# Output tiles in a pool of their own, the second unit's queries in the scores' banks, and a half's row products earlier

## The chip, the core and the metric

The kernel runs on one core of one Trainium2 chip. The metric is the device time of one execution in microseconds (us); lower is better. The engines are PE (TensorE), DVE (VectorE), ACT (ScalarE), POOL (GpSimd) and SP (SyncE, which here issues DMAs only). They run beside each other and wait for one another by semaphores. PSUM, into which PE writes, has eight banks.

## The reference, cut to what matters

Two layers, each an attention and a feed-forward network (FFN), each followed by a residual and a layer norm; two sequences of 1024 tokens, 256 features. The first attention is grouped-query softmax attention with rotary positions, the first FFN a gated one with int8 weights. The second attention is a gated delta rule with 16 heads of 128, and the last FFN has sign weights. The change touches the end of the first FFN, and the delta rule:

```python
q = silu(dwconv_causal(x @ Wq, ...))          # 4 taps; k and v in the same way
alpha, beta = sigmoid(x @ Wa + ba), sigmoid(x @ Wb + bb)
def step(S, inp):                              # per head, over T
    err = einsum('bhvk,bhk->bhv', S, kt) - vt
    S = at[..., None, None] * S - bt[..., None, None] * err[..., None] * kt[:, :, None, :]
    return S, einsum('bhvk,bhk->bhv', S, qt)
o = (o - mu) * rsqrt(var + 1e-05) * ln_w + ln_b      # per head
o = (o * sigmoid(x @ Wg)).reshape(B, T, H * DV)
x = layernorm(x + o @ Wo)
```

## The kernel before, in words

**Stages.** The first attention takes up to about 680 us. The second half of the first FFN (blocks n = 8 to 14, two row tiles of 128 tokens each) then runs beside the key work of the delta rule's first units. From about 820 to 2010 us the delta rule's 32 units follow, some 37 us each; the last FFN runs beside the last two and behind them.

**Units.** The tokens are cut into four halves (each 512 tokens, HC = 4 chunks of 128; the names `hi`, HT = 512), the 16 heads into NS = 8 pairs (HP = 2 heads). Unit i is pair s = i mod 8 of half hi = i // 8. For a unit, `project` makes a 512-column product (two heads, six matmuls each, float32 split into high and low parts), for v, q, k and the output gate g. `conv` reads it from PSUM: ACT writes the last tap and two DVE operations (L275) add two taps; `conv_out` lets ACT write the fourth tap (`far`, L289), POOL add it (L292) and ACT apply silu. Only when `far` has read the bank is it free. `keys` does this for k, four units ahead (AHEAD), and then the decay scans (L325), the products of keys and the triangular inverse (`blocks`, `levels`: L384 and L390 on DVE, n L423, px L431 on PE). `others` does v, q, the transposed keys, the gate and the scores of the next unit. `decayed` multiplies k and q by the decays dg (POOL, L519 and L521), which a broadcast DMA loads (L214).

**The recurrence.** `recur(i)` goes over four chunks: pr is v transposed plus k times the state M (L673, L677), ACT copies it (prs, L680), pw is the inverse times prs (L688), ACT copies it (wc, L691), pm updates the state (L700, copied by DVE at L705 or added at L707), po is the output (L715, L716), which ACT copies to o.

**Finish.** `finish(i)` runs in the unit that follows unit i's own. The moments of each head (L657, L658) and a reciprocal root (om, L931 to L943, the last twelve operations on POOL) scale o (L609, three quarters of it on POOL); PE transposes it (pt, L615), ACT and DVE apply norm and gate (y, L619), POOL splits it (yh L623, yl L917), and PE multiplies by Wo (pf, 12 matmuls for two chunks). DVE adds pf to the rows `xtok` (L636). After the last pair of a half (s = NS - 1: units 7, 15, 23 and 31, so the work falls into units 8, 16, 24) the rows are normed by `layernorm` (L948 to L952) and stored on SP.

**Order.** TensorE's order is strict from the first unit on: `te.link` puts a dependency on the matmul before. The order itself is made when the kernel is built: `Places` holds generators, each yielding the place at which it goes on (UNIT = 120 places a unit), and the one with the lowest place is run next. The four places of `finish` are those of the transposes of the two heads and of the two pf products:

```python
AT_FINISH, AT_FINISH_LAST, AT_HALF = (41, 51, 101, 111), (31, 41, 71, 76), ((22, 30, 46), (1, 6, 13))
```

The other engines' orders are made by a scheduler from the dependencies, with some operations set ahead (`tc.high_priority`) or behind others (`after`).

**Memory.** `ps_p` (two banks) takes the projections, `ps_m` (two) the scores, the key products and transposes, "c" (two), "t" (one) and "l" (one) the recurrence, finish and inverse. `open_late` opens the last three and the pools "late" and "w" when the first FFN's blocks are all issued; their SBUF lies where the first FFN's tiles, its rows x among them, lay, so a first writer waits for the last reader there, the store of x.

**The start of the first unit.** `rest_of_first` loads dg of unit 0, multiplies its k and q, then runs v and q of unit 1 and both heads of key unit 4, all in `ps_p`. The last FFN block's `layernorm` uses POOL (`eng=nc.gpsimd`), then SP stores the rows (L927), then issues dg (L214).

Of the kernel before, what the change touches and what calls it, by code (L numbers as in the profile page):

```python
# [12 lines left out]
F32R = mybir.dt.float32r  # L13
# [76 lines left out]
AT_FFN = 24  # L90
AT_FINISH, AT_FINISH_LAST, AT_HALF = (41, 51, 101, 111), (31, 41, 71, 76), ((22, 30, 46), (1, 6, 13))

FFN0, FFN1, FFN1_LAST, FFN1_TAIL = 7.6, 22.0, 27.0, 40.0
# [51 lines left out]
def delta_rule(  # L145
# [24 lines left out]

    def open_late():
        pools["late"] = open_pool(right, "dlate", "right", 2)
        pools["w"] = open_pool(outer, "dw", "right")
        for name, bufs in (("c", 2), ("t", 1), ("l", 1)):
            pools[name] = open_pool(right, "ps_" + name, "right", bufs, PSUM)
# [62 lines left out]

    def project(m, i, h):
        hi, s = place(i)  # L240
        if h == 0 and ("w" + m) not in st[i]:
            st[i]["w" + m] = weights(m, s)
        wh, wl = st[i]["w" + m]
        xh, xl = halves[hi]["xh"], halves[hi]["xl"]
        pp = bank(ps_p, "p", "pp")
        hs = slice(h * P, (h + 1) * P)
        for k in range(2):
            mm3(pp, wh[:, k, hs], wl[:, k, hs], xh[:, k, :], xl[:, k, :], k == 0, k == 1)
        return pp
# [10 lines left out]
    def conv(m, i, h, pp):  # L260

        hi, s = place(i)
        n, hd = "qkv".index(m), s * HP + h
        acc = half_tile(early if m == "k" else conv_pool, m, 10 if m == "k" else 4)
        st[i][m, h] = acc

        with tc.high_priority():
            nc.scalar.activation(  # L268
                acc, pp, AF.Identity, bias=cb[:, n, hd : hd + 1], scale=cw[:, n, hd, KS - 1 : KS]
            )  # L270
            if hi % 2 == 0:
                nc.scalar.copy(halos[:, n, hd, :], pp[:, HT - KS + 1 :])  # L272

            for d in range(1, KS - 1):
                made = nc.vector.scalar_tensor_tensor(  # L275
                    acc[:, d:], pp[:, 0 : HT - d], cw[:, n, hd, KS - 1 - d : KS - d], acc[:, d:], ALU.mult, ALU.add
                )
                if m == "k" and d == 1 and solved:
                    after(made, solved[-1])
        return made  # L280
# [18 lines left out]
    def keys(i, t0):  # L299

        hi, s = place(i)
        col = halves[hi]["col"]
        pps = [project("k", i, h) for h in range(HP)]
        if i < last:
# [175 lines left out]

    def pair(m, i):

        pps = [project(m, i, h) for h in range(HP)]
        for h in range(HP):
            conv(m, i, h, pps[h])
        if i < last:
            yield AT_OUT
        for h in range(HP):
            conv_out(m, i, h, pps[h])
# [32 lines left out]

    def gate(i):
        st[i]["pg"] = [project("g", i, h) for h in range(HP)]

    def gate_rows(i):
        for h in range(HP):
            g = half_tile(pools["late"], "gt", 5)
            made = nc.scalar.activation(g, st[i]["pg"][h], AF.Tanh, scale=0.5)
# [28 lines left out]
    def rest_of_first():  # L558
# [4 lines left out]
        te.strict, te.last = True, ended[0]  # L563
        for m in "vq":
            drain(pair(m, 1))
        ks = keys(AHEAD, AT_KEYS)
        next(ks)
        lines.add(ks, next(ks), 0)

    def gate_of_first():  # L570
        gate(0)
        yield GAP
        gate_rows(0)

    def finish(i, o, m, chunks, places):

        hi, s = place(i)
        if s == 0:
            halves[hi]["x"] = load_tokens(pools["late"], hi * HC, HC)
        x = halves[hi]["x"]  # L580
        if chunks[0] == 0:
            st[i]["wo"] = []
            for part in range(2):
                t = pools["late"].tile([P, HP, E], F32R, name=f"wo{part}", tag=f"wo{part}", bufs=1)
                nc.sync.dma_start(
# [25 lines left out]
        for h in range(HP):  # L611
            yield places[h]
            pt = bank(pools["t"], "t", "pt")[:, 0 : nc_ * P]
            for c in chunks:
                te.link(nc.tensor.transpose(pt[:, (c - c1) * P : (c - c1 + 1) * P], o[:, c, h, :], ident))  # L615
            y = half_tile(pools["late"], "y", 1)[:, 0 : nc_ * P]
            with tc.high_priority():
                nc.scalar.activation(pt, pt, AF.Identity, bias=lnb, scale=lnw)
                nc.vector.scalar_tensor_tensor(y, st[i]["gt", h][:, t1], 1.0, pt, ALU.add, ALU.mult)  # L619
            yh = pools["late"].tile([P, HT], F32R, name="yh", tag="yh", bufs=2)[:, 0 : nc_ * P]  # L620
            yl = pools["late"].tile([P, HT], F32R, name="yl", tag="yl", bufs=2)[:, 0 : nc_ * P]
            with ahead():
# [21 lines left out]
    def recur(i):  # L644
# [8 lines left out]
        def moments(c):  # L653
# [6 lines left out]
            if c % part == part - 1:  # L660
# [3 lines left out]
                    i, o, m[:, chunks[0] * HP : (c + 1) * HP, :], chunks,  # L664
                    AT_HALF[c // part] if i == last else AT_FINISH_LAST if i == last - 1 else AT_FINISH,
                ), at, at if i == last else (i + 1) * UNIT)
# [178 lines left out]
    for i in range(-AHEAD, last + 1):  # L845
# [19 lines left out]
        elif 0 <= i < last:  # L865
            lines.add(others(i + 1), t + AT_ROWS, t)
        if i == 0:
            lines.add(gate_of_first(), t + AT_QUERIES)
        if i >= 0:
# [28 lines left out]
def tile_two_layers(ctx: ExitStack, tc: tile.TileContext, a, out):  # L898
# [586 lines left out]
    def open_ffn(group):  # L1485
# [20 lines left out]
        def block(n):  # L1506
# [45 lines left out]
            with tc.high_priority() if n == NT - 2 else nullcontext():  # L1552
                for i in range(2):
                    y = new("fy", [P, E], 2)
                    nc.vector.tensor_mul(y, po[i], s_down)
                    nc.vector.tensor_add(x[:, n + i, :], y, x[:, n + i, :])
                anchor["norm"] = layernorm(pool, x, n, 2, eng=nc.gpsimd)
                store_tokens(xs, n, x[:, n : n + 2, :])
# [129 lines left out]
```

## Time and profile before

| | us |
|---|---|
| median of 3 runs | 2052.26 (2052.05 to 2056.88) |
| the profiled execution, its time | 2052.92 |
| its span, first to last instruction | 2051.2 |
| mean granted clock of TensorE | 0.977 |
| 800 to 840: PE busy of 40 us | 30.7 |
| 1110 to 1165: PE busy of 55 us | 49.30 |
| 1185 to 1240 (no half ends here) | 51.72 |
| 1405 to 1460 | 45.46 |
| 1700 to 1755 | 51.33 |

The profiled execution gives the durations; 1.7 us of its time lie outside the span. In the lines, a number behind "<-" in brackets is the idle time just before an instruction, with the instruction that ended it. The line numbers are those of the kernel before. In a window of 55 us in the middle of a half PE is busy for 51.7; the three windows in which a half ends show how much PE stands there.

### The profile page before, as it was taken

To read this page: it belongs to the slowest core of one execution; us is meant where nothing else is said; L and a number is where in the kernel's file an instruction comes from. 1 tells how busy PE (TensorE), PEld (TensorE's weight loads), DVE (VectorE), ACT (ScalarE), POOL (GpSimd) and SP (SyncE) were. 2 spreads that over 40 slices of the span, in tenths; PEclk is the share of its full clock that TensorE was granted. 3 is DMA by queue.
4 is the path that set the end of the run, shared out by engine and by line. 5 is a ranking of instruction groups with operands and counts; after the bars stand their busy time and mean duration, and the time that the engine had idled before them with its cause. 6 is when DMAs were issued, how large, how long until landed. Compare 5 with 4: busy or idle time off the path is not lost.

```text
span 2051.2 us, 49222 instructions
## 1 busy us (share of the span) xinstructions
PE 1888.1 (92%) x18657; PEld 1491.8 (73%) x18657; DVE 1475.0 (72%) x3477; ACT 1266.7 (62%) x2731; POOL 1077.4 (53%) x1739
## 2 busy tenths in 40 slices
PE   5898889999998898999999899999899999999986
PEld 3454455555556787888889789888888888888775
DVE  5756666887756995676787787678678679766566
ACT  1365556566655366567676676776676766676542
POOL 4353333331124464666776656666567676665453
PEclk8999999999999999899999999999999999999997
DMA  5564443441232431443444434345434344443010
GB/s 169 165 190 133 147 131 125 149 135 55 69 77 62 116 92 55 134 123 110 127 115 116 142 99 118 115 115 137 116 101 133 114 126 109 125 135 96 18 52 22
DMA packets 312998, 229.17 MB, mean 112 GB/s; under 512 B 139640, under 2 KB 278904, under 8 KB 312760
## 3 DMA queue, kind: packets, MB, share of 16 engines
q1 hardware_dynamic: 299640, 210.73, 35.3%
q10 hardware_dynamic: 9760, 10.83, 1.6%
q0 software_dynamic: 3360, 4.46, 0.9%
q8 instruction: 147, 2.41, 0.5%
q14 instruction: 91, 0.75, 0.1%
HBM read 171.18 MB, written 51.87 MB: 109 GB/s over the span
## 4 chain that ended last, share of the span: by engine, by line
PE 57%; DVE 11%; DMA 6%; ACT 5%; POOL 4%; issue 3%; SPq 1%; DVEq 0%; ACTq 0%; POOLq 0%
PE pp L968 5%; PE pp L969 4%; PE pp L970 4%; PE ps L1342 4%; PE av L1363 4%; PE ps L1273 3%; PE pkq L508 3%; PE pm L700 2%; PE pr L677 2%; DVE at L325 2%; PE pw L688 2%; PE po L716 2%; PE po L715 2%; PE p L478 2%; PE p L471 2%
## 5 line engine op out<-in xcount | busy, mean ns | idle before, releaser
L1282 DVE TENSOR_REDUCE mx<-ps 128x4 f32<-128x1024 f32 (+1 forms) x320 | 344.2, 1111 | 130.1 <-PE ps L1273 89.3
L1346 ACT ACTIVATE es<-ps 128x512 f32<-128x512 f32 (+1 forms) x608 | 313.9, 578 | 127.2 <-PE ps L1342 116.7
L1342 PE MATMUL ps<-qT,kT 128*128 128x512 f32 (+3 forms) x768 | 219.1, 368 | 19.2 <-ACT es L1346 18.4
L1273 PE MATMUL ps<-kT,qT 128*128 128x512 f32 x576 | 200.0, 421 | 28.1 <-DVE mx L1282 18.1
L1342 PEld LDWEIGHTS ps<-qT,kT 128*128 128x128 f32 x768 | 129.6, 188 | 105.2 <-ACT es L1346 59.6
L1273 PEld LDWEIGHTS ps<-kT,qT 128*128 128x128 f32 x576 | 101.8, 191 | 88.7 <-DVE mx L1282 48.0
L289 ACT ACTIVATE far<-pp,cw 128x509 f32<-128x509 f32 x192 | 133.2, 699 | 46.6 <-DVE k L275 18.8
L1363 PE MATMUL av<-es,vaug 128*32 128x512 f32 (+3 forms) x1536 | 156.7, 496 | 0.7 <-POOL es L1349 0.7
L917 POOL TENSOR_TENSOR wfl<-wf,wfh 128x256 fp32r<-128x256 f32 x80 | 58.4, 733 | 187.2 <-ACT wfh L1006 155.9
L1349 POOL TENSOR_SCALAR_AFFINE_SELECT es<-es 128x512 f32<-128x512 f32 x128 | 80.2, 635 | 145.3 <-ACT es L1346 141.7
L275 DVE SCALAR_TENSOR_TENSOR q<-pp,cw,q 128x511 f32<-128x511 f32 (+1 forms) x128 | 93.2, 742 | 47.6 <-ACT halos L272 24.2
L275 DVE SCALAR_TENSOR_TENSOR k<-pp,cw,k 128x511 f32<-128x511 f32 (+1 forms) x128 | 92.1, 743 | 45.5 <-ACT k L268 25.0
L292 POOL TENSOR_TENSOR q<-q,far 128x509 f32<-128x509 f32 x64 | 69.3, 1085 | 97.8 <-ACT far L289 97.7
L275 DVE SCALAR_TENSOR_TENSOR v<-pp,cw,v 128x511 f32<-128x511 f32 (+1 forms) x128 | 92.2, 739 | 33.4 <-ACT v L268 18.3
L292 POOL TENSOR_TENSOR k<-k,far 128x509 f32<-128x509 f32 x64 | 77.7, 1215 | 51.2 <-ACT far L289 50.6
L519 POOL TENSOR_TENSOR k<-k,dg 128x508 f32<-128x508 f32 x64 | 82.2, 1284 | 33.0 <-PE pkq L508 29.0
L1006 ACT CAST wfh<-wf 128x256 fp32r<-128x256 f32 x80 | 32.3, 405 | 107.4 <-DMA wf<-in_w1k 35.7
L716 PE MATMUL po<-wc,at 128*128 128x128 f32 x512 | 96.8, 276 | 0.0
L680 ACT COPY prs<-pr 128x256 f32<-128x256 f32 x128 | 48.8, 381 | 77.7 <-PE pr L677 69.5
L325 DVE TENSOR_TENSOR_SCAN at<-da,d 128x512 f32<-128x512 f32 x64 | 90.1, 1448 | 0.0
L700 PE MATMUL pm<-wc,kc 128*128 128x128 f32 x448 | 77.6, 296 | 11.4 <-ACT wc L691 11.4
L688 PEld LDWEIGHTS pw<-prs,lt 128*128 128x128 f32 x512 | 76.7, 191 | 14.9 <-ACT prs L680 3.0
(323 smaller groups left out, 5916.2 us busy)
## 6 DMA issues: line engine op xcount, KB each, us to landing
wk<-w1k SPq DMA_DIRECT2D x64, 256.0 KB
da<-dec SPq DMA_DIRECT2D x64, 256.0 KB
wv<-w1v SPq DMA_DIRECT2D x64, 256.0 KB
wq<-w1q SPq DMA_DIRECT2D x64, 256.0 KB
dg<-dec SPq DMA_DIRECT2D x64, 256.0 KB
wg<-w1g SPq DMA_DIRECT2D x64, 256.0 KB
wo<-w1o SPq DMA_DIRECT2D x64, 256.0 KB
ad<-avs ACTq DMA_DIRECT2D x32, 256.0 KB
```

Of the source, the lines that this page charges most:

```text
L275: made = nc.vector.scalar_tensor_tensor(acc[:, d:], pp[:, 0 : HT - d], cw[:, n, hd, KS - 1 - d : KS - d], acc[:, d:], ALU.mult, ALU.add)
L289: made = nc.scalar.activation(far[:, w], pp[:, w], AF.Copy, scale=cw[:, n, hd, 0:1])
L292: nc.gpsimd.tensor_add(acc[:, KS - 1 :], acc[:, KS - 1 :], far[:, w])
L325: nc.vector.tensor_tensor_scan(e, dec, d1.rearrange("p c t -> p (c t)"), 0.0, ALU.mult, ALU.add), taps
L688: te.link(nc.tensor.matmul(pw[:, r], lhsT=lt[:, h * HC + c, :], rhs=prs[:, r], start=True, stop=True))
L700: te.link(nc.tensor.matmul(pm[:, r], lhsT=st[i]["kc", h][:, c, :], rhs=wc[:, r], start=True, stop=True))
L716: te.link(nc.tensor.matmul(po[:, r], lhsT=st[i]["at", h][:, t], rhs=wc[:, r], start=(M is None), stop=True))
L1273: anchor["mm"] = te.link(nc.tensor.matmul(ps[:, j - j0, :].rearrange("p (g k) -> p g k", k=P), lhsT=q_, rhs=kT[:, :, j * P : (j + 1) * P], ...
L1282: nc.vector.tensor_reduce(mx[:, it, j0 // 2, :], ps[:, 0:n, :].rearrange("p j (g k) -> p g j k", k=P), AX.XY, ALU.max)
L1342: te.link(nc.tensor.matmul(ps[:, g - g0, :], lhsT=kT[:, g, jb * P : (jb + 1) * P], rhs=qT[:, i0 : i0 + w], start=True, stop=True,))
L1346: exps.append(nc.scalar.activation(es[:, g0 : g0 + n, 0:w], ps, AF.Exp, scale=D ** -0.5))
L1363: mm = te.link(nc.tensor.matmul(av[ROW * g : ROW * (g + 1), i0 - ih * 512 : 512], lhsT=vaugs[b][:, jb, kv, :], rhs=es[:, g, 0:w], start=(j ...
```

## The change

A pool "out" is opened before "late" and takes the output side's tiles: the gate gt, the rows xtok, wo, y, yh and yl. `project`, `pair` and `gate` take a pair of pool and tag for their banks: q of unit 1 and the gate of unit 0 go to `ps_m`. `rest_of_first` projects only the first key head of unit 4; the second comes from a new stream, `first_keys`, at a place inside unit 0. The last FFN block's norm makes its reciprocal root on DVE (nine operations, L936 to L938) instead of POOL (twelve, L940 to L943), and one tap of unit 1's q is ordered behind that norm. `finish` of the last pair of the first three halves has its two row products at places 86 and 94 instead of 101 and 111.

The number of matmuls stays. On PE the order changes at four spots: two transposes (pr of unit 0's first chunk) go ahead of the second key head, and in units 8, 16 and 24 the sequence "k head, pw, pf, po of chunk 3, pf" becomes "pf, k head, pf, pw, po". On SP one load of wk goes ahead of the store of x, and the loads of wk in those three units come behind the two DMAs of the inverse.

```diff
@@ -89,6 +89,7 @@
 AT_LEVELS = 43, 53, 73, 83, 103, 113, 132, 142
 AT_FFN = 24
 AT_FINISH, AT_FINISH_LAST, AT_HALF = (41, 51, 101, 111), (31, 41, 71, 76), ((22, 30, 46), (1, 6, 13))
+AT_FINISH_ROWS = 41, 51, 86, 94
 
 FFN0, FFN1, FFN1_LAST, FFN1_TAIL = 7.6, 22.0, 27.0, 40.0
 
@@ -169,6 +170,8 @@
     ps_m = open_pool(left, "ps_m", "left", 2, PSUM)
 
     def open_late():
+
+        pools["out"] = open_pool(right, "dout", "right", 2)
         pools["late"] = open_pool(right, "dlate", "right", 2)
         pools["w"] = open_pool(outer, "dw", "right")
         for name, bufs in (("c", 2), ("t", 1), ("l", 1)):
@@ -236,13 +239,13 @@
 
         return divmod(i, NS)
 
-    def project(m, i, h):
+    def project(m, i, h, psum=None):
         hi, s = place(i)
         if h == 0 and ("w" + m) not in st[i]:
             st[i]["w" + m] = weights(m, s)
         wh, wl = st[i]["w" + m]
         xh, xl = halves[hi]["xh"], halves[hi]["xl"]
-        pp = bank(ps_p, "p", "pp")
+        pp = bank(*(psum or (ps_p, "p")), "pp")
         hs = slice(h * P, (h + 1) * P)
         for k in range(2):
             mm3(pp, wh[:, k, hs], wl[:, k, hs], xh[:, k, :], xl[:, k, :], k == 0, k == 1)
@@ -275,6 +278,8 @@
                 made = nc.vector.scalar_tensor_tensor(
                     acc[:, d:], pp[:, 0 : HT - d], cw[:, n, hd, KS - 1 - d : KS - d], acc[:, d:], ALU.mult, ALU.add
                 )
+                if m == "q" and i == 1 and d == 1:
+                    after(made, anchor["norm"])
                 if m == "k" and d == 1 and solved:
                     after(made, solved[-1])
         return made
@@ -300,7 +305,8 @@
 
         hi, s = place(i)
         col = halves[hi]["col"]
-        pps = [project("k", i, h) for h in range(HP)]
+        pps = [st[i].pop("first")] if "first" in st[i] else [project("k", i, 0)]
+        pps.append(project("k", i, 1))
         if i < last:
             st[i + 1]["wk"] = weights("k", place(i + 1)[1])
         for h in range(HP):
@@ -478,9 +484,9 @@
                     te.link(nc.tensor.matmul(p4[A, u, :], lhsT=n3[Z, u, :], rhs=lt[Z, u, Z], start=True, stop=True))
             nc.scalar.copy(st[i + n]["lt"][A, :, Z], p4[A])
 
-    def pair(m, i):
-
-        pps = [project(m, i, h) for h in range(HP)]
+    def pair(m, i, psum=None):
+
+        pps = [project(m, i, h, psum) for h in range(HP)]
         for h in range(HP):
             conv(m, i, h, pps[h])
         if i < last:
@@ -520,12 +526,12 @@
         if "q" in which:
             nc.gpsimd.tensor_mul(q, q, gs)
 
-    def gate(i):
-        st[i]["pg"] = [project("g", i, h) for h in range(HP)]
+    def gate(i, psum=None):
+        st[i]["pg"] = [project("g", i, h, psum) for h in range(HP)]
 
     def gate_rows(i):
         for h in range(HP):
-            g = half_tile(pools["late"], "gt", 5)
+            g = half_tile(pools["out"], "gt", 5)
             made = nc.scalar.activation(g, st[i]["pg"][h], AF.Tanh, scale=0.5)
             if copied:
                 after(made, copied[-1])
@@ -561,14 +567,21 @@
             for h in range(HP):
                 decayed(0, h, which)
         te.strict, te.last = True, ended[0]
-        for m in "vq":
-            drain(pair(m, 1))
+
+        for m, psum in (("v", (ps_p, "p")), ("q", (ps_m, "m"))):
+            drain(pair(m, 1, psum))
+        st[AHEAD]["first"] = project("k", AHEAD, 0)
+
+    def first_keys():
+
         ks = keys(AHEAD, AT_KEYS)
         next(ks)
-        lines.add(ks, next(ks), 0)
+        yield AT_ROWS + AT_OUT
+        yield next(ks)
+        yield from ks
 
     def gate_of_first():
-        gate(0)
+        gate(0, (ps_m, "m"))
         yield GAP
         gate_rows(0)
 
@@ -576,12 +589,12 @@
 
         hi, s = place(i)
         if s == 0:
-            halves[hi]["x"] = load_tokens(pools["late"], hi * HC, HC)
+            halves[hi]["x"] = load_tokens(pools["out"], hi * HC, HC)
         x = halves[hi]["x"]
         if chunks[0] == 0:
             st[i]["wo"] = []
             for part in range(2):
-                t = pools["late"].tile([P, HP, E], F32R, name=f"wo{part}", tag=f"wo{part}", bufs=1)
+                t = pools["out"].tile([P, HP, E], F32R, name=f"wo{part}", tag=f"wo{part}", bufs=1)
                 nc.sync.dma_start(
                     out=t.bitcast(F32),
                     in_=w1d["o", part][s * HP * P : (s + 1) * HP * P, :].rearrange("(h p) e -> p h e", p=P),
@@ -613,12 +626,12 @@
             pt = bank(pools["t"], "t", "pt")[:, 0 : nc_ * P]
             for c in chunks:
                 te.link(nc.tensor.transpose(pt[:, (c - c1) * P : (c - c1 + 1) * P], o[:, c, h, :], ident))
-            y = half_tile(pools["late"], "y", 1)[:, 0 : nc_ * P]
+            y = half_tile(pools["out"], "y", 1)[:, 0 : nc_ * P]
             with tc.high_priority():
                 nc.scalar.activation(pt, pt, AF.Identity, bias=lnb, scale=lnw)
                 nc.vector.scalar_tensor_tensor(y, st[i]["gt", h][:, t1], 1.0, pt, ALU.add, ALU.mult)
-            yh = pools["late"].tile([P, HT], F32R, name="yh", tag="yh", bufs=2)[:, 0 : nc_ * P]
-            yl = pools["late"].tile([P, HT], F32R, name="yl", tag="yl", bufs=2)[:, 0 : nc_ * P]
+            yh = pools["out"].tile([P, HT], F32R, name="yh", tag="yh", bufs=2)[:, 0 : nc_ * P]
+            yl = pools["out"].tile([P, HT], F32R, name="yl", tag="yl", bufs=2)[:, 0 : nc_ * P]
             with ahead():
                 (nc.gpsimd.tensor_copy if i < last else nc.scalar.copy)(yh, y)
                 sub_low(nc.gpsimd if i < last else nc.vector, yl, y, yh)
@@ -662,7 +675,8 @@
                 at = i * UNIT + 3 * GAP * (c + 1) + 3
                 lines.add(finish(
                     i, o, m[:, chunks[0] * HP : (c + 1) * HP, :], chunks,
-                    AT_HALF[c // part] if i == last else AT_FINISH_LAST if i == last - 1 else AT_FINISH,
+                    AT_HALF[c // part] if i == last else AT_FINISH_LAST if i == last - 1
+                    else AT_FINISH_ROWS if s == NS - 1 else AT_FINISH,
                 ), at, at if i == last else (i + 1) * UNIT)
 
         for c in range(HC):
@@ -865,6 +879,7 @@
         elif 0 <= i < last:
             lines.add(others(i + 1), t + AT_ROWS, t)
         if i == 0:
+            lines.add(first_keys(), t + AT_ROWS, t)
             lines.add(gate_of_first(), t + AT_QUERIES)
         if i >= 0:
             lines.add(recur(i), t, chain=True)
@@ -1554,7 +1569,7 @@
                     y = new("fy", [P, E], 2)
                     nc.vector.tensor_mul(y, po[i], s_down)
                     nc.vector.tensor_add(x[:, n + i, :], y, x[:, n + i, :])
-                anchor["norm"] = layernorm(pool, x, n, 2, eng=nc.gpsimd)
+                anchor["norm"] = layernorm(pool, x, n, 2, eng=nc.gpsimd if n < NT - 2 else None)
                 store_tokens(xs, n, x[:, n : n + 2, :])
             yield 0.2
 
```

## The prediction

> **What bounds the kernel now.** I read the page first: busy shares, then the span in forty slices.
>
> ```profile
> span 2051.2 us, 49222 instructions
> PE 1888.1 (92%) x18657; PEld 1491.8 (73%) x18657; DVE 1475.0 (72%) x3477; ACT 1266.7 (62%) x2731; POOL 1077.4 (53%) x1739
> PE   5898889999998898999999899999899999999986
> PEclk8999999999999999899999999999999999999997
> ```
>
> TensorE bounds the whole, in an order written out by hand. The change leaves its number of matmuls as it is, so it can only move the time in which PE stands still or runs at a lowered clock. A slice is 51 us; two stretches that the change touches are dips: slice 16 (769 to 821 us, PEclk 8), where the delta rule's first unit begins, and the half boundaries (units 8, 16, 24). The stage table and PE's waits at the transition:
>
> ```profile
> 810.00:820.00 10.00, 5.97 (x19) 4.01 (x19) 7.55 (x20) 6.06 (x13) 5.02 (x13) 0.74 0.41 122
> 820.00:830.00 10.00, 7.34 (x26) 5.69 (x25) 9.37 (x28) 3.60 (x9) 8.95 (x8) 0.50 0.99 313
> 830.00:840.00 10.00, 9.98 (x59) 8.65 (x58) 1.66 (x8) 5.00 (x16) 1.63 (x3) 0.90 0.40 93
> ```
>
> Columns: PE, PEld, DVE, ACT, POOL busy, granted clock, DMA share, GB/s. In 820 to 830 the clock is 0.50. PE's waits of 800 to 832 (sum, times, longest):
>
> ```profile
> PE pp L968 <- ACT far L289: 5.8, 3, 2.1
> PE pr L677 <- DVE M L705: 0.9, 1, 0.9
> ```
>
> PE waits three times for a projection bank that the convolution's last tap (far) still reads. The timelines of DVE, POOL and SP there name the rest:
>
> ```profile
> 813.67 1.15 DVE L952 TENSOR_SCALAR x<-x,ln 128x256 f32<-128x256 f32 x1 [1.05 <-POOL ln L943]
> 815.40 0.40 DVE L952 TENSOR_SCALAR x<-x,ln 128x256 f32<-128x256 f32 x1
> 822.59 4.02 DVE L325 TENSOR_TENSOR_SCAN at<-da,d 128x512 f32<-128x512 f32 x2
> 820.91 1.26 POOL L519 TENSOR_TENSOR k<-k,dg 128x508 f32<-128x508 f32 x1 [2.49 <-DMA dg<-dec]
> 815.83 0.36 SPq L927 DMA_DIRECT2D xs<-x  x1
> 816.29 0.90 SPq L214 DMA_DIRECT2D dg<-dec  x2
> ```
>
> The last FFN block's norm ends late (12 POOL operations at a pitch of 0.28, 809.42 to 813.64), so its store is issued at 815.83; dg is queued behind it on SP and lands at 820.87; POOL's four dg multiplications end at 827.6; DVE meanwhile is in two scans, with the copy of M (L705) behind them. The boundaries, from PE's waits:
>
> ```profile
> PE px L431 <- DVE n L423: 2.3, 1, 2.3
> PE pt L615 <- POOL o L609: 7.7, 2, 7.1
> ```
>
> The first is of 1110 to 1165, the second of 1405 to 1460. PE is busy 49.30, 45.46 and 51.33 of 55 us at the three boundaries, against 51.72 in 1185 to 1240: room of about 2.4, 6.3 and 0.4.
>
> **The change, part by part: the transition.**
>
> Pool of their own. The first prs copy (L680) no longer inherits x's store; at 821.0 the store and pr (820.04) were both behind it. Alone about 0 to 1. The tanh's gt now waits for the store, but it stands at 833 and later: nothing.
>
> Second unit's queries in ps_m. Today v and q of unit 1 and key head 0 and 1 take the two ps_p banks in turn: waits of 1.82, 1.92 and 2.11, the 5.8 above. With q in the two ps_m banks and the first key head straight behind, I add up from v's end at 806.55: q 12 matmuls at 0.235 (2.8) to 809.35, key head 0 (6, 1.4) to 810.75. All three waits go from this place. The first pr then waits for silu and taps of v, which end on POOL at 810.97 and ACT about 812.85; key head 1, moved behind it, ends at 814.5; pw, wc and pm end by 816.3 (today 823.6). That is 7 us earlier, but what comes next is pr with M of chunk 1, and it needs k multiplied by dg.
>
> Norm on DVE. Nine operations of 0.15 to 0.17 at a pitch of about 0.1 (0.9), plus two x of 0.40, replace twelve at 0.28 (3.4) that were interleaved with two adds of 1.08. The norm ends at about 810.9 rather than 815.8, the store goes then, and dg behind it at 811.4. Issue to landing took 4.6 (816.29 to 820.87) with the channel still 41% busy, so dg lands at about 816.0 to 816.5. The ordering of q's tap behind the norm costs DVE nothing, since that tap waits for ACT anyway.
>
> The dg multiplications. On POOL two at 1.26 and the next at 1.27 to 2.17: both heads of k are done at 821.3 to 821.8 (with the q between them) against 827.63. M's copies now stand ahead of the scans on DVE (about 817.4, today 826.65). So pr with M of both heads moves from 828.48 to about 821.8: gain 6.7. Two things are late next. POOL's adds of q's far taps are queued behind the dg work, ACT's far of the keys behind them, and wc of chunk 1 behind that, at about 827; and gate of unit 0, now in ps_m, must be read by ACT before pk takes the bank. They take back about 1.1: pr of chunk 2 at 830.1 rather than 835.69. **Gain 5.6.** Bounds: 3 if dg takes 2 us longer to land (the wg and wk loads are issued closer behind it; 313 GB/s at 0.99 in 820 to 830 shows the channel full) and half a us more goes to ACT; 8 if none of the 1.1 is taken back and wg runs at full clock.
>
> On that clock: matmuls of wg took 0.43 from 828 to 832 and 0.23 after, following four waits of 0.9 to 2.1 each within 20 us. The change gathers these into one wait of 4 to 5 us for dg, so I keep the twelve wg matmuls slow before and after, a difference of 0. The Trainium skill, TensorE: Matmul & The Clock Gate, section What's actually happening, says the clock halves after one idle window of about 3.4 us. By that rule the old gaps would not have throttled, which this trace contradicts (0.50), and the new one would; the sum by the rule would be about 2.4 us less gain (12 times 0.20).
>
> SP. One wk load goes ahead of the store (0.6 of issue); ps_p and PE's queue wait for neither. Nothing.
>
> **Part by part: the half boundaries.** AT_FINISH_ROWS moves both output products (pf, 12 matmuls each) of units 7, 15, 23 ahead of the following k products and pw: about 15 places, 4 to 5 us. PE's count is the same. The first pf meets yl's second head (POOL L917 ends 1120.27; PE is there at about 1118.5): a wait of 1.1 to 1.7, paid three times, but the following pf and pr would have waited on DVE partly anyway; I carry it inside the sums below. The wk loads behind d and dt on SP come ten places later and are needed a unit on: nothing. The store of the half is earlier, good for the next gates, which are not waited for.
>
> DVE is the matter: at 1130 to 1150 it is busy 10.0 of every 10 us. The scheduled order puts the row norm of the first two chunks (add, statistics, nine short operations at 0.08 pitch, two scalings at 0.40: about 3 us) ahead of the k taps. Then the head norm (om, L931 to L933) stands behind more work than today. First boundary: three v taps (2.1), L339 (0.67), two M updates (0.59), L407 (0.70), 12 short row-norm operations (1.0), two L952 (0.80), about 5.7 us more. Third: the same with a second L339 and two statistics, 6.6. Second: three taps, two L339, L407 leave, the row norm comes, 3.1 less. Behind om stand 12 POOL operations at 0.29, o (L609), then pt (L615), and PE in strict order behind pt:
>
> ```profile
> 1133.13 0.17 DVE L933 TENSOR_SCALAR om<-om 128x8 int32<-128x8 int32 x1
> 1137.83 2.48 POOL L609 TENSOR_SCALAR o<-o,om 128x128 f32<-128x128 f32 x3
> 1147.05 1.58 PE L431 MATMUL px<-n,dt 32*32 32x32 f32 x128 [2.26 <-DVE n L423]
> 1439.25 0.26 POOL L943 TENSOR_TENSOR om<-om 128x8 f32<-128x8 f32 x1
> 1439.62 2.60 POOL L609 TENSOR_SCALAR o<-o,om 128x128 f32<-128x128 f32 x3
> ```
>
> First: o ends 6 to 6.7 later, so pt, today at 1139.98 without a wait, waits some 6; the 2.26 that px waits today is swallowed, so px is 4.5 later. Third: pt 6.5 later, px's wait 0.8, so 5.8 later. Second: the om chain on POOL is no longer split by q's two adds (1435.52, 1438.21), o ends at about 1437.0 instead of 1442.2, matmuls behind a shorter wait run faster (L420 1.93 there, 1.29 at the first): 6.9 earlier. **Sum +3.4**, slower. Bounds: -7 (first and third cost 0, second gains all), +12 (first 6.7, third 6.5, clock loss of 1 each as after the 7.1 wait, second gains 2).
>
> **Sum.** The profiled run took 2052.92 (span 2051.2 and 1.7 around it), 0.66 over the median. 2052.92 - 5.6 + 3.4 = 2050.7; less 0.66, 2050.
>
> **Rivals.**
>
> Faster, boundaries lose nothing: the row norm of some 6 us runs on DVE before the taps instead of between them and px's n, where the same 6 us delay PE today; the wait only changes place. For it: all DVE work ahead of n is the same within 2 us by count. Against: the strict order has pt between. Then -5.6 - 6.9, 2040; with half the cost left, 2045.
>
> Slower, the wait for o takes the place of px's: first +6.7, third +6.5, about 1 each for the clock that falls after such a wait, second 0 because POOL's adds of v still stand in the om chain, transition only 3 because dg lands late. +15.2 - 3 = +12.2, 2064. It decides if the boundaries cost over 12 with the full gain, or 9 with 3. For it: PE's 7.1 wait for L609 at the second boundary shows that the chain does end there. Against: work moved ahead of om is absent later.
>
> No gain at the start: the 5.8 of bank waits turns into a wait for dg or for wc, whose landing does not move. Then +3.4: 2055.7. Against: the store's place on SP is plain.
>
> **How the numbers follow.** A difference of 0.3% (6.2 us) is about what a measurement can tell: 2046 to 2058. Forecast case 0.36, its own range 2046 to 2056; no gain at the start 0.04; boundaries free 0.34, 2038 to 2046; wait for o 0.26, 2058 to 2066. The eight-in-ten range cuts the ends of the last two: 2040 to 2062. Faster 0.34, within 0.40, slower 0.26.
>
> **What would show it.** Right: no wait of pp L968 at 806 to 818; store issued near 811, dg landing near 816; pr of chunk 1 with M at 822, of chunk 2 at 830; at the first and third boundary a PE wait of 5 to 6 at pt L615 for POOL o L609, and the second's 7.1 down to 2. Wrong: waits at pt below 2 everywhere (then faster), dg later than 818, or a wait of the first pf over 2.

## The result and the profile after

The changed kernel is slower: its median is 2059.26 us over 14 runs against 2054.26 us of the kernel before over 14 runs; their ratio is 1.0032, with a 95% interval of 1.0021 to 1.0044. That is 6.6 us (4.3 to 9.0), where 2.3 us less were forecast. The profiled execution took 2057.25 us, its span 2055.5.

The page of the changed kernel, by the same lines as before:

```profile
span 2055.5 us, 49215 instructions
PE 1889.2 (92%) x18657; PEld 1492.2 (73%) x18657; DVE 1477.7 (72%) x3486; ACT 1268.0 (62%) x2731; POOL 1074.4 (52%) x1727
PE   5898899999998997999999899999999997999896
PEclk8999999999999999899999999999999999999997
```

PE has the same matmuls and is busy for 1 us more. Slices 16 (the start) and 23 (the first half end) are dips in both, slice 34, where the third half ends, is a new one, and slice 29, at the second half end, is no dip any more. The view is too coarse for the sizes; the stretches below are not.

To see where the time went I take marks that both traces have: the start of the last pair of fhh casts (ACT's rounding of the first FFN's hidden rows), pr of unit 0's third chunk (chunk 2, counted from 0), and the first pr of units 8, 10, 16, 18, 24, 26 and 31. The stretches between them:

| stretch | before | after | difference | forecast |
|---|---|---|---|---|
| up to the last fhh cast (unchanged code) | 799.97 | 797.19 | -2.8 | 0 |
| start: to pr of unit 0's chunk 2 | 35.72 | 32.53 | -3.2 | -5.6 |
| units 1 to 7 | 259.09 | 259.56 | +0.5 | 0 |
| first half end, units 8 and 9 | 76.88 | 82.15 | +5.3 | +4.5 |
| units 10 to 15 | 217.81 | 219.35 | +1.5 | 0 |
| second half end, 16 and 17 | 80.20 | 75.28 | -4.9 | -6.9 |
| units 18 to 23 | 218.37 | 216.42 | -2.0 | 0 |
| third half end, 24 and 25 | 73.32 | 82.98 | +9.7 | +5.8 |
| unit 26 to the end of the span | | | +0.2 | 0 |

The first row is scatter between executions (over all profiles below that mark lies between 797 and 810 us, in code that no edit touches); without it the sum is +7.1, close to the 6.6 of the timed runs. Each stretch is of one execution of a kernel, and code that no edit aims at scatters too: over all traces below, units 1 to 7 take 259.1 to 261.3 us, and unit 26 to the end 288.2 to 295.2.

PE's waits at the start (800 to 835) and the stage table of the changed kernel:

```profile
PE pr L691 <- POOL k L525: 7.2, 2, 4.9
PE pk L503 <- ACT gt L535: 1.0, 1, 1.0
PE pw L702 <- ACT prs L694: 0.7, 1, 0.7
```

```profile
810.00:820.00 10.00, 2.50 (x12) 1.72 (x12) 9.79 (x25) 1.92 (x4) 4.25 (x3) 0.76 0.89 269
820.00:830.00 10.00, 8.49 (x41) 7.25 (x42) 4.60 (x22) 6.15 (x15) 7.63 (x10) 0.73 0.54 163
```

The 5.8 us of bank waits are gone, and 7.2 us of waits for POOL's products with dg stand in their place. PE is busy for 2.5 us of ten there. Over the whole start stretch PE stands idle for 10.6 us (9.3 before) and is busy for 21.9 (26.4 before) with the same matmuls, at a granted clock of 0.84 (0.71 before). So by PE's account the 3.2 us are not saved waits: the waits grew by 1.3, and the matmuls took 4.5 less because fewer of them ran at half clock. The timelines of SP, POOL and PE:

```profile
809.72 0.91 SPq L217 DMA_DIRECT2D dg<-dec  x2
815.75 1.39 POOL L525 TENSOR_TENSOR k<-k,dg 128x508 f32<-128x508 f32 x1 [7.88 <-DMA dg<-dec]
817.20 0.80 PE L691 MATMUL pr<-M,k 128*128 128x128 f32 x2 [4.90 <-POOL k L525]
820.55 0.80 PE L691 MATMUL pr<-M,k 128*128 128x128 f32 x2 [2.34 <-POOL k L525]
821.99 0.63 PE L985 MATMUL pp<-x2h,wg 128*128 128x512 f32 x1
822.42 0.63 PE L983 MATMUL pp<-x2h,wg 128*128 128x512 f32 x1
```

dg is used 6.0 us after its issue, where 4.6 were taken, and the wg products follow one another at 0.43 us (starts 821.99 and 822.42).

The first half end, PE's waits in 1105 to 1162 of the changed kernel, and then DVE, POOL and PE in time:

```profile
PE pt L628 <- POOL o L622: 4.2, 2, 2.6
PE pm L714 <- ACT wc L705: 1.9, 1, 1.9
PE pp L983 <- ACT far L294: 1.3, 1, 1.3
PE pf L985 <- POOL yl L932: 1.0, 1, 1.0
```

```profile
1130.89 0.16 DVE L946 TENSOR_SCALAR om<-om 128x8 f32<-128x8 f32 x1
1132.29 0.67 DVE L947 TENSOR_SCALAR om<-om 128x8 int32<-128x8 int32 x1
1134.78 0.16 DVE L948 TENSOR_SCALAR om<-om 128x8 int32<-128x8 int32 x1
1141.17 1.22 POOL L297 TENSOR_TENSOR q<-q,far 128x509 f32<-128x509 f32 x1
1142.38 0.98 POOL L622 TENSOR_SCALAR o<-o,om 128x128 f32<-128x128 f32 x1
1143.41 0.47 PE L628 MATMUL pt<-ident,o 128*128 128x128 f32 x1 [1.59 <-POOL o L622]
1144.67 1.93 PE L426 MATMUL p<-ll,lo 32*32 32x32 f32 x128
```

From the first to the last of the three operations of om on DVE pass 3.9 us, with v's taps and M's updates between; L948 comes 45.5 us after the unit's first pr (38.4 before), POOL's last o behind q's add, and pt waits 2.59, 0.32 and 1.59 us. Behind those waits the 128 small products of p take 1.93 us rather than 1.29, and the px wait of 2.26 is gone: the wait has moved and grown, and px starts 61.2 us after the unit's first pr (52.3 before). The third half end, waits in 1700 to 1757, shows the same with L948 at 47.4 us:

```profile
PE pt L628 <- POOL o L622: 5.4, 2, 4.3
```

The longer waits are not all. Behind them the granted clock (the last but two of the numbers) is 0.50 in both ends:

```profile
1143.00:1149.60 6.60, 6.19 (x147) 5.79 (x148) 2.17 (x6) 2.48 (x8) 3.29 (x4) 0.50 0.47 160
1734.00:1743.00 9.00, 6.38 (x147) 5.58 (x148) 4.17 (x12) 4.35 (x10) 6.39 (x7) 0.50 0.43 147
```

The matmuls are the same before and after, so I put what PE is busy longer down to the clock, and what it is idle longer to waits (us; "half clock" is the time at 0.50):

| half end | idle before, after | busy before, after | half clock before, after | difference: idle, busy |
|---|---|---|---|---|
| first | 5.7, 9.4 | 71.2, 72.8 | 3.4, 6.8 | +3.7, +1.6 |
| second | 9.5, 5.9 | 70.7, 69.4 | 10.2, 0 | -3.7, -1.2 |
| third | 3.7, 10.3 | 69.7, 72.7 | 0, 10.2 | +6.7, +3.0 |

Of the 10.1 us at the three ends 6.7 are waits and 3.4 are the clock. The prediction named the waits' mechanism; the clock it had only in a bound and a rival.

### The profile page after: what moved, and what is told of

It is laid out like the page before. It is cut to its first block, busy times and chain, and to the rows that moved or that the text cites. A ratio compares the mean times of both kernels' runs of the same rounds, so it can differ in the third digit from the quotient of the medians.

```text
span 2055.5 us, 49215 instructions
## 1 busy us (share of the span) xinstructions
PE 1889.2 (92%) x18657; PEld 1492.2 (73%) x18657; DVE 1477.7 (72%) x3486; ACT 1268.0 (62%) x2731; POOL 1074.4 (52%) x1727
## 4 chain that ended last, share of the span: by engine, by line
PE 58%; DVE 11%; DMA 6%; ACT 5%; POOL 4%; issue 2%; SPq 1%; DVEq 0%; ACTq 0%; POOLq 0%
PE pp L983 5%; PE pp L985 4%; PE pp L984 4%; PE ps L1357 4%; PE av L1378 4%; PE ps L1288 3%; PE pkq L514 3%; PE pm L714 2%; PE pw L702 2%; PE pr L691 2%; PE po L730 2%; PE po L729 2%; PE p L484 2%; PE p L477 2%; PE ph L1536 1%
## 5 line engine op out<-in xcount | busy, mean ns | idle before, releaser
L1288 PE MATMUL ps<-kT,qT 128*128 128x512 f32 x576 | 199.5, 420 | 27.9 <-DVE mx L1297 18.5
L278 DVE SCALAR_TENSOR_TENSOR q<-pp,cw,q 128x510 f32<-128x510 f32 (+1 forms) x128 | 93.1, 743 | 44.8 <-ACT q L271 22.5
L297 POOL TENSOR_TENSOR q<-q,far 128x509 f32<-128x509 f32 x64 | 69.4, 1087 | 91.0 <-ACT far L294 90.9
L1021 ACT CAST wfh<-wf 128x256 fp32r<-128x256 f32 x80 | 32.5, 406 | 103.1 <-DMA wf<-in_w1k 34.6
L691 PE MATMUL pr<-M,k 128*128 128x128 f32 x448 | 82.9, 280 | 13.4 <-POOL k L525 7.2
L729 PE MATMUL po<-M,q 128*128 128x128 f32 x448 | 88.3, 279 | 0.0
```

Source lines behind the costliest of these rows:

```text
L278: made = nc.vector.scalar_tensor_tensor(acc[:, d:], pp[:, 0 : HT - d], cw[:, n, hd, KS - 1 - d : KS - d], acc[:, d:], ALU.mult, ALU.add)
L297: nc.gpsimd.tensor_add(acc[:, KS - 1 :], acc[:, KS - 1 :], far[:, w])
L691: te.link(nc.tensor.matmul(pr[:, r], lhsT=st[i]["k", h][:, t], rhs=M[:, r], start=False, stop=True))
L729: te.link(nc.tensor.matmul(po[:, r], lhsT=st[i]["q", h][:, t], rhs=M[:, r], start=True, stop=False))
L1288: anchor["mm"] = te.link(nc.tensor.matmul(ps[:, j - j0, :].rearrange("p (g k) -> p g k", k=P), lhsT=q_, rhs=kT[:, :, j * P : (j + 1) * P], ...
```

## The experiments

Theory A: the start gains, and the half ends lose because the row norm now stands ahead of the head norm om on DVE, so that o comes after PE has reached pt. Rival B: PE's new order itself (the early product that waits for yl) is the loss. Rival C: the start costs later. Rival D, taken up when the parts did not add: the start and the early rows hurt each other otherwise. Each experiment compares with the kernel before on the same chip; the stretches are of one trace a run.

**The start alone.**

```diff
-AT_FINISH_ROWS = 41, 51, 86, 94
+AT_FINISH_ROWS = 41, 51, 101, 111
```

> The change without its earlier row products (places 101 and 111 as before). Theory A (the start gains, the loss is all at the half boundaries): counted from the first v product of unit 1, unit 1 starts 3 us sooner than before and stays so; 0.9985 of before, about 3 us less. Rival C (the start's new order costs something later, in the units behind it): PE's lead of 3 us is given back by unit 31, ratio 1.000 or above.

Measured: 0.9973 (0.9958 to 0.9988). The start stretch is 33.6 us (35.7), and nothing of it is given back: C falls.

**The rows alone**, on the kernel before.

```diff
-                    AT_HALF[c // part] if i == last else AT_FINISH_LAST if i == last - 1 else AT_FINISH,
+                    AT_HALF[c // part] if i == last else AT_FINISH_LAST if i == last - 1
+                    else AT_FINISH_ROWS if s == NS - 1 else AT_FINISH,
```

> The kernel before with only the earlier row products (places 86 and 94). In the built order 3.0 us more DVE work stands ahead of the head norm (om) at the first and third boundary, and 3.6 us less at the second, against 4.8, 2.9 less and 5.5 in the whole change. Theory A (what counts is the DVE work ahead of om): first +3, second -6, third +4, sum about +1, ratio 1.0005. Theory B (what counts is PE's order: the early product waits for yl and the later stall loses its cover): as in the whole change, +5.3, -4.9, +9.7, sum +10, ratio 1.005.

Measured: 0.9988 (0.9973 to 1.0003); half ends -1.5, -4.5, +2.6 against before. The -1.5 at the first end is no gain of this order: the trace before had 3.4 us at half clock there, this one none. Where the kernel before and others with its places ran at full clock, the first or third end took 72.1 to 73.3 us (table below), so 75.3 is 2 to 3 us more. That is Theory A's +3 in size, but not its cause: the early products cost as much with om at its old place (74.7 and 75.2, next run), so om's 3.7 us more cost little here. Neither part alone makes the kernel slower, but both together do. PE's waits in 1110 to 1165:

```profile
PE pf L972 <- POOL yl L919: 1.0, 1, 1.0
PE pt L616 <- ACT o L607: 0.9, 1, 0.9
PE pt L616 <- POOL o L610: 0.8, 1, 0.8
```

The wait for yl is the same 1.0, that for o is small: B does not carry the loss of the whole change. om's last DVE operation is at 42.1 us and o ends 49.3 us after the unit's first pr, while PE is at pt from 47.0.

**Row norm behind om**, the rest as in the whole change (early products).

```diff
-                if s == NS - 1:
+                if i == last:
                     layernorm(gx, x, c1 + c0, 2, eng=nc.gpsimd if i == last and not final else None)
...
+        if s == NS - 1 and i < last:
+            yield UNIT + 6
+            for c0 in range(0, nc_, 2):
+                layernorm(gx, x, c1 + c0, 2, behind=anchor["om"])
```

(`behind` puts the statistics after the third operation of om.)

> The whole change, with the row norm (statistics, root, scaling) of the three half ends ordered behind the head norm om on DVE; the row products stay at places 86 and 94. DVE work ahead of om is then 1.0, 5.9 and 0.7 us less than before. Theory A: first boundary -1, second -7, third -1, with the start's -3.2 about -12, ratio 0.994. Theory B: the boundaries stay at +10, ratio 1.003. In between if both act.

Measured: 0.9960 (0.9944 to 0.9977), the half ends 74.7, 74.1 and 75.2. Against the whole change (82.2, 75.3, 83.0) that is -7.4, -1.2 and -7.8. PE's waits in 1105 to 1162 have no pt any more:

```profile
PE pm L719 <- ACT wc L710: 1.4, 1, 1.4
PE px L437 <- DVE n L429: 1.3, 1, 1.3
PE pf L993 <- POOL yl L937: 1.0, 1, 1.0
```

The early products are still there and the loss is not, so the row norm's place on DVE carries it.

**The same with the products late** (places 101 and 111).

> The change's start, the row products at places 101 and 111 as before, and the row norm behind om. DVE work ahead of om is 1.1, 5.4 and 1.1 us less than before. Theory A: first -1, second -6, third -1 and the start's -3.2: about -11, ratio 0.9946, within 0.1% of the kernel with early products and the same row norm. Theory B: the boundaries as before, -3.2, ratio 0.9985.

Measured: 0.9938 (0.9918 to 0.9958); half ends 72.7, 74.6, 72.7. Against the early products with the same norm: -2.0, +0.4, -2.5. First and third ends ran at full clock in both, and PE waits at pt for o in neither. So PE's new order does cost some 2 us at the first and third end, of which 1.0 is the wait for yl.

**Places 91 and 101** in the whole change.

```diff
-AT_FINISH_ROWS = 41, 51, 86, 94
+AT_FINISH_ROWS = 41, 51, 91, 101
```

> The whole change, the row products at places 91 and 101 instead of 86 and 94. In the built order 1.9 us more DVE work stands ahead of om at the first and third boundary and 4.9 less at the second (whole change: 4.1 and 4.8 more, 3.6 less, without the nine operations of the start), and the early product still waits for yl. Theory A with a threshold (PE meets pt some 47 us after the unit's first pr; o must be there by then): first -1, second -5, third +2, as with the rows alone, start -2: about -6, ratio 0.997. Theory D (start and early rows hurt each other by something other than the place of om): the loss stays, ratio 1.003.

Measured: 0.9951 (0.9935 to 0.9968), half ends 74.7, 73.6, 74.5. Five places later, with om's last operation at 40.3 us, the loss is gone.

**The whole change, with the last FFN block's root on POOL**, 300 us ahead of the first half end.

```diff
-                anchor["norm"] = layernorm(pool, x, n, 2, eng=nc.gpsimd if n < NT - 2 else None)
+                anchor["norm"] = layernorm(pool, x, n, 2, eng=nc.gpsimd)
```

> The whole change with places 86 and 94, only the last FFN block's root back on POOL (at 800 to 820 us, far from the half boundaries). In the built order 3.0 and 3.2 us more DVE work then stand ahead of om at the first and third boundary and 4.0 less at the second, much as with the rows alone (3.0, 3.0, 3.6 less). Theory A: the boundaries are those of the rows alone (-1.5, -4.5, +2.6), start -2: about -5, ratio 0.9975. Theory B or D (places 86 and 94 together with the start cost the time themselves): +5, ratio 1.0025.

Measured: 0.9976 (0.9960 to 0.9992), half ends 75.7, 75.7, 78.0, om at 42.2, 39.1 and 41.6 us. The places 86 and 94 and the queries' banks are still there, and the loss is not: D in the sense of a contest on the chip falls. The edit at the start reached the half ends through the scheduler that orders DVE when the kernel is built: at the first end M's two updates (L721) and a transposition (L413) stand ahead of om's last operation in the whole change and behind it in this kernel, which differs in that one line.

All first and third half ends, ordered by where om's last DVE operation stands (us after the first pr of units 8 and 24). The last column is the time at half clock in the first and the third end:

| kernel | om | first end | third end | half clock |
|---|---|---|---|---|
| norm behind om, late products (three kernels, two of them below) | 36.0 to 36.1 | 72.7 to 72.8 | 72.7 | 0, 0 |
| norm behind om, early products | 38.2, 38.2 | 74.7 | 75.2 | 0, 0 |
| before | 38.4, 38.4 | 76.9 | 73.3 | 3.4, 0 |
| start alone | 38.3, 38.4 | 72.9 | 72.1 | 0, 0 |
| start alone, root on POOL (below) | 38.4, 38.3 | 75.9 | 75.3 | 3.4, 3.4 |
| start alone, queries in the projections' banks (below) | 38.3, 38.3 | 75.0 | 72.6 | 3.4, 0 |
| second key head only (below) | 38.4, 38.4 | 72.1 | 73.1 | 0, 0 |
| start alone, no pool of its own (below) | 38.4, 38.4 | 75.6 | 72.7 | 3.4, 0 |
| places 91 and 101 | 40.3, 40.3 | 74.7 | 74.5 | 0, 3.4 |
| rows alone | 42.1, 42.2 | 75.3 | 75.9 | 0, 3.4 |
| whole, root on POOL | 42.2, 41.6 | 75.7 | 78.0 | 0, 6.8 |
| whole change | 45.5, 47.4 | 82.2 | 83.0 | 6.8, 10.2 |

The entries with om at 38.3 and 38.4 have the same places of the row products. They split by the clock: seven at full clock take 72.1 to 73.3 us, five with 3.4 us at half clock 75.0 to 76.9. Why the clock falls in one and not in the other is not shown. With earlier products and at full clock om at 38 to 42 us gives 74.7 to 75.7, so up to 42 us its place costs less than this scatter shows. With om at 45 and 47 us the ends are 6.5 to 8.3 us longer than that: 4 to 5.5 of it waits, 2.5 to 3 the clock. That reads as a threshold, o in time for PE at pt or not; the step lies between 42 and 45 us, and the whole change alone has entries beyond it.

**Four runs on the start.** The measure is the stretch from the last fhh cast to pr of the third chunk: 35.7 before, 33.6 with the start alone. Each of the four ran once (2057.6, 2052.8, 2056.6 and 2052.0 us, beside medians of 2057.6 and 2057.0 before), so only the stretch speaks. It scatters by about 1 us: the whole change's start took 32.5 in its own trace and 33.5 to 33.7 in the four other kernels with the same start.

Root on POOL again (the edit of the last diff, on the start alone):

> The start alone (rows at 101 and 111), with the last FFN block's root back on POOL. Measured from the last fhh cast to pr of unit 0's third chunk: 35.7 us before, 33.6 with the start alone. If the norm's end, the store and dg behind it set the start: 35.5 to 36.5. If the bank waits did: 33.6.

Measured: 33.4; the gain stays, against the first expectation, so the norm's place did not give it. But dg was not late again: it is issued at 819.50, 14.1 us after the fhh cast, where the start alone has 14.3 and the kernel before 16.3. That dg's earlier issue gave the gain is not refuted by this run.

Unit 1's queries again in the projections' banks:

```diff
-        for m, psum in (("v", (ps_p, "p")), ("q", (ps_m, "m"))):
+        for m, psum in (("v", (ps_p, "p")), ("q", (ps_p, "p"))):
```

> The start alone, with unit 1's queries in the projections' two banks as before (the norm on DVE, the second key head still behind pr). If dg's landing sets the start: 33 to 34 us from the last fhh cast to pr of the third chunk, although PE waits some 4 us for banks before. If the bank waits set it: 35.7.

Measured: 32.7, with 5.4 us of bank waits, so these were not on the path here. Undoing either part leaves the gain; what both kernels keep is the second key head behind pr, and an issue of dg 2 to 3 us earlier than before (13.3 us after the cast here).

The second key head behind pr, nothing else (first_keys on the kernel before, all banks and the root as before):

> The kernel before with one part of the start: the second key head of unit 4 behind pr of unit 0, all in the projections' two banks, the root on POOL, no pool of their own. In the built DVE order M's copies then stand ahead of the two scans, the rest as before. If the place of M's copies gave the start's gain: 33.5 us from the last fhh cast to pr of the third chunk (35.7 before). If the bank waits, the norm or the pool gave it: 35.5 or more.

Measured: 32.4, as much as the whole start with one part of it, and with dg issued as late as before (16.3 us after the cast). PE, DVE and POOL there:

```profile
822.62 0.63 PE L977 MATMUL pp<-x2l,wk 128*128 128x512 f32 x1
823.05 0.63 PE L978 MATMUL pp<-x2h,wk 128*128 128x512 f32 x1
827.31 0.48 DVE L712 COPY M<-pm 128x128 f32<-128x128 f32 x2
827.84 4.30 DVE L326 TENSOR_TENSOR_SCAN at<-da,d 128x512 f32<-128x512 f32 x2
828.89 2.17 POOL L520 TENSOR_TENSOR k<-k,dg 128x508 f32<-128x508 f32 x1
831.11 0.49 PE L684 MATMUL pr<-M,k 128*128 128x128 f32 x2 [2.52 <-POOL k L520]
832.37 0.39 PE L977 MATMUL pp<-x2l,wg 128*128 128x512 f32 x1
832.59 0.39 PE L978 MATMUL pp<-x2h,wg 128*128 128x512 f32 x1
```

M's copies stand ahead of the scans now. pr with M comes 26.4 us after the fhh cast; in the whole change it comes at 23.4. But there wg runs at 0.43 (2.3 us for twelve products more than the 0.23 here), and pk waits 1.0 for gt, which sits in the scores' banks: the 3 us of lead are gone by the third chunk. Before, that pr (of the second head) came at 27.9, so 1.5 of the 3.3 us gained here are made up to it. The rest is made behind it, where wg ran at full clock. That M's place gave the 1.5 fits the lines; no run moves M alone.

Without the outputs' own pool:

> The start alone without the outputs' own pool (gt, xtok, wo, y, yh, yl again in the pool of the recurrence). The first prs copy waits for the store of x again; in the built DVE order M's copies stand behind the two scans. If either sets the start: 34.5 to 35.7 us from the last fhh cast to pr of the third chunk; if dg's landing alone does: 33.6.

Measured: 33.9, with M's copies behind the scans and only 1.2 us of waits for M. So M's place is not the only way to the gain: with the bank waits gone the scans start 18.9 us after the fhh cast (22.6 before), M is done at 22.7 and dg's products at 24.5. That the meeting of late scans with copies behind them is what has to go fits all of these runs, but is not shown by one that changes it alone. The pool by itself is worth no more here than the scatter (33.9 against 33.5 to 33.7).

**Two versions that were to be better yet**: dg's loads ahead of the store of x, on top of the start with the norm behind om.

```diff
-        decays(0)
+        with tc.high_priority():
+            decays(0)
```

> The kernel with the start and the row norm behind om (places 101 and 111), and unit 0's dg loads ahead of the store of x on SP. If the loads are held by the store's place alone, dg lands 1 to 2 us sooner and pr of the third chunk comes 32.0 instead of 33.7 us after the last fhh cast: ratio to before 0.993. If dg waits for the memory under it or the channel, 33.7 and 0.994.

Measured: 31.4 for the start stretch, 2.3 less, and 0.9928 (0.9907 to 0.9949), the fastest here by its ratio, though not told apart from 0.9938. dg was held by its place on SP: it is issued 13.5 us after the cast instead of 14.4, and its first product starts 1.0 us sooner.

The same, with queries and gate in the projections' banks:

> The kernel with the row norm behind om and dg ahead of the store, with unit 1's queries and unit 0's gate back in the projections' two banks. In the whole change PE stood 4.9 and 2.3 us for dg's products and the twelve wg matmuls behind ran at 0.43 us; with only the second key head moved they ran at 0.235. If shorter waits spread over the start keep the clock, pr of the third chunk comes 29 to 30 us after the last fhh cast (31.4 with the queries in the scores' banks), ratio to before 0.992. If the bank waits cost their own time, 32.5 to 33.5, ratio 0.9935.

Measured: 35.1 for the stretch, 0.9942 (0.9922 to 0.9962). The expectation failed: key head 0 waited 3.58 us for its bank and pm 2.30, wg ran at 0.43 again. Bank waits that were worth nothing in one kernel (32.7 against 33.6) go with 3.7 us in this one.

## Why the prediction was wrong, point by point

**The second term, the half ends, had the mechanism and not the size.** The prediction named the row norm ahead of om, the chain om, o, pt on PE, and the three signs; it said +4.5, -6.9, +5.8, and it was +5.3, -4.9, +9.7. The step that failed is "the 2.26 that px waits today is swallowed, so px is 4.5 later", and its like at the third end: px was to come 4.5 and 5.8 us later at the first and third end, and came 8.9 and 11.2 later, of which 3.6 and 1.5 were won back behind it. Two terms of that step were too small. The chain: om's last DVE operation moved by 7.1 and 9.0 us, where the count of work had 5.7 and 6.6, and the waits for yl and far were new, the first of them carried "inside" without a number; the early products by themselves cost some 2 us an end. At the third end PE waited in the new kernel 1.05 (yl), 1.32 (far), 1.31 (wc), 0.95 (M), 4.30 and 1.10 (o), 10.0 in all, against 3.2 before. And the clock: PEclk fell to 0.91 over 1700 to 1755 (1.00 before); the prediction's own case has no term for it, only its bound and its slower rival (1 us each). That the first end came close to its forecast (+5.3 for +4.5) is luck: the trace before had lost some 3 us to the clock there (76.9, against 72.1 to 73.3 for the same order at full clock), and against the full clock the change cost 9 to 11 us at both ends. The px wait of 2.26 that was to be swallowed was of that one end too; at the third end before it was 0.77, with the start alone 0.76 and 0.78. Measured over the three ends, waits cost 6.7 us where 3.4 were summed, and the clock 3.4 where nothing was. The rival "the wait for o takes the place of px's" has 15.2 for the first and third end, and measured are 15.0, but that is luck in part: it had 7.7 and 7.5 where 5.3 and 9.7 came, and no gain at the second end, which did gain.

**The first term, the start, gave 3.2 where 5.6 were summed.** The step that failed is "dg lands at about 816.0 to 816.5": counted from the fhh cast, the issue was at 12.5 and the first use at 18.6, which on before's clock is 818.5, with the channel 0.89 busy. So pr with M of the second head came 1.5 us later than summed (823.3 instead of 821.8). Another 0.9 went behind it, where "They take back about 1.1" was too little: the wait for gt alone was 1.0. The prediction's own lower bound, 3 if dg lands 2 us late, is what came. As for the causes, the bank waits and the norm's place were not needed: undoing either leaves the gain. The second key head alone gave as much, but in another way, more than half of it behind pr at full clock. How the 3.2 divide among dg's issue, M's place and the clock stays open.

**The clock.** wg was kept slow in both, and it was (0.43). The Trainium skill, TensorE: Matmul & The Clock Gate, section What's actually happening, has the clock halved by one idle window of about 3.4 us; the 4.9 us wait with wg at 0.43 behind it agrees. The kernel with the second key head moved does not: there the products of wk ran at 0.43 behind waits that were none above 1.9 us, and wg at 0.23 right behind one of 2.5.

**Right:** the store at the front with dg behind it, PE's wait for dg of some 5 us, the second end's relief, and no wait of PE for wk there.

**The cover that was not seen.** The forecast read the built order of the half ends as a property of the places 86 and 94. It was a property of the whole build: root on POOL or places 91 and 101 give other DVE orders, and a faster kernel. That the prediction's order was right for this build is why its signs held; the row norm ahead of om is the same cause in both readings.

## What to carry to other kernels

Where a scheduler orders an engine at build time, an edit at one end of a kernel can reorder a busy engine 300 us later; compare the built order of the saturated engine at each stage, and price the chain that the strict engine waits for, from its first operation to the wait, and price the clock behind that wait (here a third of the loss at the half ends). Work that nobody waits for (here the row norm) belongs behind the chain that somebody does, by an explicit order: that order made the whole change 0.9960 instead of 1.0032. A wait that is removed has a gain only if what follows it on the path does not wait for something else: 5.4 us of bank waits were worth nothing with the start alone, and stood beside a loss of 3.7 us with dg first. And when two traces of one stretch are compared, compare their granted clock first: half ends of the same order differed by up to 4.8 us, and split by it.

## What the runs showed of the hardware

Two scans on DVE took 2.33 us (whole change, at 1125.19) to 4.30 us (beside POOL's products with dg, second key head only); a POOL product with dg took 1.26 us alone and 2.17 beside a scan. In the half ends of all traces the granted clock was 1.00 or 0.50, and 0.50 lasted 3.4, 6.8 or 10.2 us in a piece; 3.4 us of it went with about 1.6 us more of PE's busy time for the same matmuls (71.1 to 71.3 against 69.5 to 69.7 us). In the first 800 us, which no edit touches, executions differ by up to 12 us in the last fhh cast (797.2 to 809.5), about twice the 6.6 us that the change cost.
